# Extra products from constants in TensorE's planned pauses (a two-layer adaLN network, one core)

## Chip, core and metric

One core of a Trainium2 chip. The metric is the time of one execution in microseconds on the device. Times of several executions are given as their median. Five engines work side by side, each through its own queue in order: TensorE (PE), VectorE (DVE), ScalarE (ACT), GpSimd (POOL) and SyncE (SP), which here issues most DMAs.

## What is computed

Two layers on x of shape (16, 512, 128), float32. In each layer the input is normalised over its 128 features and scaled and shifted by amounts that depend on the batch entry; a mixer is applied; the result is multiplied by a gate and added.

```python
mod = (_silu(L0_c) @ L0_wmod).reshape(16, 6, 1, -1)        # sa, ca, ga, sb, cb, gb
h = _layernorm(x) * (1 + ca) + sa
x = x + ga * linear_attention(h)      # 16 heads of 8, causal, features elu + 1
h = _layernorm(x) * (1 + cb) + sb
x = x + gb * channel_mix(h)           # h mixed with the token before it, sigmoid gate, relu squared
# layer 1, with its own mod
h = _layernorm(x) * (1 + ca) + sa
x = x + ga * retention(h)             # 16 heads, decay, norm of each head, silu gate
h = _layernorm(x) * (1 + cb) + sb
y = _layer_norm(h + attention(h)) * g1 + be1    # over the batch entries of one time step, 4 heads
z = y + experts(y)                    # 8 experts, each token goes to the one of the highest logit
x = x + gb * (_layer_norm(z) * g2 + be2)
```

## The kernel before

The work has two parts. In the first, the 16 batch entries go through both layers up to the last normalisation, one entry (512 tokens) to a block. `both_layers` (L1086) is the program of one block: `linear_attention` (L857), `channel_mix` (L910), `retention` (L945). In the second, 16 blocks of another cut of the tokens go through `attention` (L1209) and `route` (L1407), which writes each token's row to the region of its expert in DRAM by an indirect DMA; `expert_tile` (L1602) then reads 256 rows of one expert at a time, applies it and writes the rows out by an indirect DMA.

The order of all instructions is fixed when the program is built. Each block is a Python generator that yields what it does next, "P1.9" for about 1.9 us of TensorE, "A0.8" for ScalarE, "V" for VectorE, "G" for GpSimd, "S" for SyncE, "D" for a delay. `queued` (L166) keeps, for every engine, the planned time up to which it is taken (`until`), picks the generator that can start first, and lets it issue its instructions. `now[0]` is the planned time. Five blocks run at once in the first part (`WIDTH`), seven in the second (`NROW`). The two parts are two calls of `queued`, the first at L1123, the second at L1756, each with a plan that starts at zero; between them the pools of the first part are closed and those of the second opened.

PSUM has eight banks, each 128 x 512 float32. `banks` (L271) takes some from the front of the list `free_banks`, `back` (L288) puts them at its end when the instruction that reads them has been issued in the plan. `bank_at(n)` (L248) makes a tile in bank n; an instruction that writes it waits for the last reader of that bank.

The start: the weights `wa_mod` (in `shared`) and `wa_sb` come on ScalarE's queue; on SyncE's queue come x of blocks 0 and 1, `wb_mod`, the vectors, the constants `con` (L320), x of blocks 2 to 4 and the rest. TensorE's first products are those of `modulation` (L428), from `wa_mod` and the conditioning; then the transposes in `turned` (L575), then, after ScalarE's scale and shift (L577), the products for queries and keys (L870). The chain that fills x of a block into ScalarE's queue is `normed` (L562).

The names of lines used below: L614 is `by_token`, four or more 128x128 products; L685 transposes keys; L817 and L799 are the products with states and values, after them come L840 (transposes in `closed`) and L849 (the sum into x by VectorE). In the second part L1231 transposes rows, L1234 copies them (`hb`), L1239 makes queries and keys, L1255 and L1257 spread the keys, L1292 makes the scores, L1342 applies them to the values, L1358 closes attention; L1633, L1646, L1666 and L1681 are an expert's transposes and products.

Of the kernel before, what the change touches and what calls it, by code (L numbers as in the profile page):

```python
# [29 lines left out]
P = 128  # L30
B, T, C = 16, 512, 128
# [4 lines left out]
NBLK = 16  # L36
# [12 lines left out]
SPACE, SPACE2 = 5.0, 5.0  # L49
# [5 lines left out]
NTILE, NW, NIN, NHID = 7, 5, 6, 3  # L55
NBANK = 8
NVAL, NATT = 3, 2
ND = P // DUO
LN_EPS = 1e-5
DEN_EPS = 1e-6  # L60
# [8 lines left out]
NROW = 7  # L69
# [93 lines left out]
        return at, self.next.endswith("-"), self.rank, self.ready  # L163


def queued(chains, apart, width, rank=lambda n: n, now=[0.0], side=(), behind=0):  # L166

    chains, whole, begin, free = iter(chains), [], 0.0, 0.0
    running = [Chain(steps, 0.0, -1) for steps in side]
    until = dict.fromkeys("PVAGS", 0.0)
    count = 0
    while True:
        while len(whole) < width and (steps := next(chains, None)) is not None:
            chain = Chain(steps, max(begin, free), rank(count))
            count += 1  # L180
            whole.append(chain)
            running.append(chain)
            begin = chain.ready + next(apart)
        if not running:
            return
        first = min(running, key=lambda chain: chain.start(until))
        now[0] = first.start(until)[0]
        if first.next:
            engine, us = first.next[0], float(first.next[1:].rstrip("-"))
            if engine in until:  # L190
                until[engine] = now[0] + us
            first.ready = now[0] + us + 0.1
        first.next = ""
        took = next(first.steps, None)
        if took is None:
            running.remove(first)
            if first in whole:
                first.ended = True
                while whole and whole[0].ended:
                    free = max(free, whole.pop(0).ready)  # L200
            elif first.of is not None:
                first.of.parts -= 1
                first.of.ready = max(first.of.ready, first.ready)
                if first.of.parts == 0:
                    running.append(first.of)
        elif isinstance(took, Begun):
            running += [Chain(steps, first.ready, first.rank + behind) for steps in took]
        elif isinstance(took, str):
            first.next = took
        else:  # L210
            first.parts = len(took)
            running.remove(first)
            running += [Chain(steps, first.ready, first.rank, first) for steps in took]
# [3 lines left out]
def tile_adaln(ctx: ExitStack, tc: tile.TileContext, x, wa, wb, vec, wex, const, out):  # L217
    nc = tc.nc
    mm = nc.tensor.matmul
# [19 lines left out]
    con = cp.tile([P, K_COS], F32, name="con")  # L239
# [8 lines left out]
    def bank_at(n):  # L248
        return p1.tile([P, T], F32, tag=f"bank{n}", name="bank")
# [10 lines left out]
    free_values, free_sets, now = [], [], [0.0]  # L260
    free_banks = list(range(NBANK))
# [26 lines left out]
    def back(*tiles):  # L288
        for t in tiles:
            free_banks.append(held.pop(id(t))[0])  # L290

    X, here, done = {}, {}, set()

# [44 lines left out]
    def v(i):  # L338
        return vec_sb[:, i : i + 1]
# [39 lines left out]
    def blanks():  # L379
        yield "G1.4"  # L380
        make_identity(nc, ident)
        nc.gpsimd.memset(lneps, LN_EPS)
        nc.gpsimd.memset(eps4, LN_EPS)
        nc.gpsimd.memset(power, -0.5)
        nc.gpsimd.memset(minus, -1.0)
        yield "G1.8"
        for t in values:
            nc.gpsimd.memset(t, 1.0)
        free_values.extend(range(NVAL))
        yield "G1.0"  # L390
        nc.gpsimd.memset(avg, 1.0 / C)
        nc.gpsimd.memset(keep, 1.0)
        nc.gpsimd.memset(keep[:, :, 0:1], 0.0)
        for n in range(NATT):
            yield "D%.1f" % (5.0 + 14.0 * n)
            yield "G1.1-"
            nc.gpsimd.memset(states[n], 0.0)
            free_sets.append(n)

    def blank_values():  # L400
        for n in range(NVAL):
            engine = nc.gpsimd if n else nc.vector
            yield "G1.1-" if n else "V1.1-"
            engine.memset(v_chunks[n], 0.0)
            yield "G2.1-" if n else "V2.1-"
            engine.memset(v_heads[n], 0.0)
            done.add(("blank", n))
            yield "D%.1f" % max(0.0, BLANKS + 8.0 * n - now[0])
# [45 lines left out]
    def gates():  # L454
        yield [
            modulation(0, wa_mod, 4.5, [(0, 1), (2, 3, 4, 5)]),
            modulation(1, wb_mod, LATER, [tuple(range(6))]),
        ]
        yield "V0.6-"
        ts(omu, mu, -1.0, 1.0, ALU.mult, ALU.add)  # L460
        gbe2 = cp.tile([P, B], F32, name="gbe2")
        ts(gbe2, mod1[:, 5, :], v(V_BE2), None, ALU.mult)
        gg2 = cp.tile([P, B], F32, name="gg2")
        ts(gg2, mod1[:, 5, :], v(V_G2), None, ALU.mult)
        shift = cp.tile([P, B], F32, name="shift")
        ts(shift, mod1[:, 3, :], v(V_BO), None, ALU.add)
        of_entry = (mod0[:, 2], mod0[:, 5], mod1[:, 2], gbe2, mod1[:, 4], shift, gg2)
        got = yield from banks(2)
        yield "P1.6"
        for n, m in enumerate(of_entry):  # L470
            nc.tensor.transpose(got[n // 4][0:B, n % 4 * C : (n % 4 + 1) * C], m, ident)
        yield "V1.2"
        mod_sb = of_set(NATT - 1, [P, RG, T], "sc").rearrange("p r t -> p (r t)")[0:B, 0 : NMOD * C]
        for n, ps in enumerate(got):
            at = slice(4 * n * C, min(NMOD, 4 * n + 4) * C)
            nc.vector.tensor_copy(mod_sb[:, at], ps[0:B, 0 : at.stop - at.start])
        back(*got)
        yield "S0.5"
        nc.sync.dma_start(out=mod_rows, in_=mod_sb)
        here["rows"] = now[0] + 2.5  # L480
        done.add("omu")
        yield "D20.0"
        for n in range(GRP):
            yield "S0.5"
            nc.sync.dma_start(out=gain[n * B : (n + 1) * B], in_=mod_rows[:, NGATE * C :])

    def end_weights():
        yield "D%.1f" % (LATER - 1.0)
        yield "V0.6-"
        nc.vector.tensor_copy(wend[:, 0], wa_col(A_PROJ))  # L490
        ts(wend[:, 1], wa_col(A_V), 0.5, None, ALU.mult)
        ts(wend[:, 2], wb_mod[:, B_O : B_O + C], 0.5, None, ALU.mult)
        done.add("wend")

    def turned_weights():
        yield "D20.0"
        yield "V0.7"
        tt(cen, ident, avg, ALU.subtract)
        ts(cen_h, blk, -1.0 / HD, None, ALU.mult)
        tt(cen_h, cen_h, ident, ALU.add)  # L500
        ps = yield from bank()
        yield "P0.4"
        nc.tensor.transpose(ps[:, 0:C], wb_col(B_V), ident)
        yield "V0.3"
        nc.vector.tensor_copy(wvt, ps[:, 0:C])
        yield "P0.5"
        mm(ps[:, C : 2 * C], lhsT=wvt, rhs=cen_h, start=True, stop=True)
        yield "V0.3"
        nc.vector.tensor_copy(wv1, ps[:, C : 2 * C])
        back(ps)  # L510
        done.add("turned")
# [563 lines left out]
    def blank_rows():  # L1075
        yield "D60.0"
        blank = con[:, K_NONE + 1 - R_END : K_NONE + 1]
        for e in range(NE + 1):
            yield "S0.7"
            nc.sync.dma_start(  # L1080
                out=sorted_rows[e * REGION : e * REGION + TS].rearrange("(p a) k -> p a k", a=2),
                in_=blank.unsqueeze(1).to_broadcast([P, 2, R_END]),
            )
            yield "D8.0"

    def both_layers(b):  # L1086
# [40 lines left out]
        lambda n: min(n, 2 * LATE - n),  # L1127
        now,
        side=[gates(), blanks(), blank_values(), end_weights(), turned_weights(), blank_rows()],
    )  # L1130
    order.close()
    blocks.close()
# [32 lines left out]
    for n in range(2):  # L1165
        t = wk.tile([P, 4 * ND, MH, DUO], F32, name=f"k_own{n}", bufs=1)
        nc.gpsimd.memset(t, 0.0)
# [575 lines left out]
    def attend_and_route(i):  # L1743
        k, n, first = of_block[i]
        row = yield from attention(i)
        if k not in logits:
            logits[k] = wk.tile([P, MOST_G, NE], F32, tag="logits", name="logits", bufs=4)[:, 0 : 4 * n]
            ready[k] = 0
        at = 4 * (i - first)
        yield from normed_rows(i, row, logits[k][:, at : at + 4])  # L1750
        ready[k] += 1
        if ready[k] == n:
            yield Begun([route(k, first, n, logits[k])])

    with tc.manual_schedule():
        queued((attend_and_route(i) for i in range(NBLK)), repeat(SPACE2), NROW, now=now, behind=4)  # L1756


# [90 lines left out]
```

## Time and profile before

| | |
|---|---|
| median of 3 runs | 1036.85 us (1034.77 to 1041.96) |
| the profiled execution, its own time | 1042.77 us |
| its span, first to last instruction | 1040.7 us |
| TensorE busy | 848.7 us (82%), 16319 records |
| VectorE, ScalarE, GpSimd busy | 722.6, 719.9, 586.7 us |
| mean granted clock of TensorE | 0.923 |
| HBM traffic | 65.94 MB read, 38.51 MB written |

The profile is of one execution. Busy time is the time in which an engine has an instruction in it; records of TensorE's products overlap a little, since they are pipelined. A row of a timeline gives the start in us, the length in us, engine and line, operation, output and inputs, the count that was merged, and in brackets how long the engine had been idle and what ended that. The granted clock is the share of full speed that TensorE was given; in the stretches of this trace it is 1.0 or 0.5. The part of the chain of waits in an engine's name is time in which that engine's work was what the end waited for.

### The profile page before, as it was taken

How to read it: one execution, taken by the hardware profiler on the slowest of the kernel's cores; microseconds unless marked ns; L12 is line 12 of the kernel's file. 1: busy time of each engine (PE TensorE's matmuls, PEld its weight loads, DVE VectorE, ACT ScalarE, POOL GpSimd, SP SyncE). 2: the span in 40 equal slices, each digit the busy share in tenths (PEclk: the TensorE clock that was granted, in tenths of full speed). 3: DMA queues.
4: the chain of work that ended last, by engine and by line, in shares of the span. 5: the costliest groups of instructions: out<-in, count | busy, mean ns of one | idle time of the engine just before them, and what ended most of it. 6: DMA issues, size and time to landing. Idle time of an engine off the chain costs nothing.

```text
span 1040.7 us, 39498 instructions
## 1 busy us (share of the span) xinstructions
PE 848.7 (82%) x16319; PEld 632.2 (61%) x16319; DVE 722.6 (69%) x2183; ACT 719.9 (69%) x1437; POOL 586.7 (56%) x782
## 2 busy tenths in 40 slices
PE   6798887888998889888888988478668678868985
PEld 4566665666766656666665656346445556646874
DVE  6466876666777778666697667658779688756454
ACT  6666676887868688876678667159768677634664
POOL 6316648544555765636375574244762575775576
PEclk9799988899999999999899889789789999978998
DMA  6634324153422333525133032230365564568763
GB/s 202 155 71 113 75 60 111 49 128 69 107 62 51 80 73 88 114 46 115 35 76 71 23 77 51 60 125 1 126 199 172 168 212 142 182 187 285 227 190 100
DMA packets 147555, 116.52 MB, mean 112 GB/s; under 512 B 75269, under 2 KB 127240, under 8 KB 147248
## 3 DMA queue, kind: packets, MB, share of 16 engines
q1 hardware_dynamic: 140720, 96.05, 35.9%
q0 software_dynamic: 6368, 17.08, 4.4%
q8 instruction: 129, 2.11, 0.9%
q10 hardware_dynamic: 288, 0.86, 0.3%
q14 instruction: 50, 0.41, 0.1%
HBM read 65.94 MB, written 38.51 MB: 100 GB/s over the span
## 4 chain that ended last, share of the span: by engine, by line
PE 35%; ACT 17%; DVE 17%; POOL 10%; issue 9%; DMA 9%; SPq 2%; POOLq 0%; another core or an unknown queue 0%; ACTq 0%; DVEq 0%
PE bank L614 5%; PE bank L1646 4%; DMA v_rows<-values 3%; PE bank L817 3%; PE bank L1666 3%; PE bank L765 3%; PE bank L799 3%; ACT q L562 3%; PE bank L780 2%; PE bank L698 2%; PE bank L870 2%; ACT kh L664 1%; POOL rs L532 1%; POOL out_x L1722 1%; DVE k_own L1255 1%
## 5 line engine op out<-in xcount | busy, mean ns | idle before, releaser
L562 ACT ACTIVATE q<-x,off,rs 128x128 f32<-128x128 f32 x244 | 100.3, 484 | 35.8 <-POOL off L559 31.6
L1722 POOL DMA_INDIRECT out_x<-z,l_to x71 | 71.9, 1013 | 38.2 <-issue 13.7
L774 ACT COPY sc<-bank 128x512 f32<-128x512 f32 x128 | 68.1, 585 | 34.5 <-PE bank L765 34.2
L747 DVE TENSOR_TENSOR sc<-bank,con 128x512 f32<-128x512 f32 x128 | 82.1, 681 | 11.3 <-PE bank L780 9.9
L765 PE MATMUL bank<-kh,q 32*32 32x128 f32 x4096 | 81.7, 281 | 9.4 <-issue 6.0
L735 POOL COPY states<-added 32x576 f32<-32x576 f32 x64 | 46.9, 732 | 67.8 <-DVE added L720 65.2
L664 ACT ACTIVATE kh<-k,con 128x512 f32<-128x512 f32 x128 | 81.8, 715 | 0.1
L1646 PE MATMUL bank<-y,w 128*128 128x256 f32 (+1 forms) x312 | 75.5, 387 | 5.6 <-ACT y L1636 3.6
L1656 ACT ACTIVATE hid<-bank,w 128x256 f32<-128x256 f32 (+1 forms) x156 | 60.4, 462 | 26.5 <-PE bank L1646 13.9
L780 PE MATMUL bank<-ident,sc 128*128 128x128 f32 x512 | 74.7, 292 | 3.2 <-DVE x L849 1.2
L765 PEld LDWEIGHTS bank<-kh,q 32*32 32x32 f32 x4096 | 60.8, 107 | 26.1 <-issue 11.2
L799 PE MATMUL bank<-v_heads,sc 128*32 128x36 f32 x4096 | 60.5, 202 | 16.4 <-issue 9.8
L1666 PE MATMUL bank<-hid,w 128*128 128x256 f32 (+1 forms) x312 | 70.6, 372 | 2.6 <-ACT hid L1656 2.2
L799 PEld LDWEIGHTS bank<-v_heads,sc 128*32 128x32 f32 x4096 | 47.3, 111 | 41.5 <-issue 25.6
L956 POOL TENSOR_TENSOR th<-th,trig 128x512 f32<-128x512 f32 x32 | 43.1, 1347 | 47.4 <-DVE th L972 41.6
L614 PE MATMUL bank<-gated,h 128*128 128x128 f32 x384 | 60.9, 309 | 10.9 <-DVE h L1018 6.7
L532 POOL TENSOR_TENSOR rs<-rs,power 128x4 f32<-128x4 f32 x64 | 66.1, 1033 | 5.0
L780 PEld LDWEIGHTS bank<-ident,sc 128*128 128x128 f32 x512 | 60.6, 149 | 11.2 <-ACT sc L774 3.8
L1646 PEld LDWEIGHTS bank<-y,w 128*128 128x128 f32 x312 | 56.4, 201 | 17.3 <-ACT y L1636 6.9
L531 POOL TENSOR_TENSOR rs<-mv,eps 128x4 f32<-128x4 f32 x64 | 17.2, 269 | 88.2 <-DVE mv L525 77.2
L614 PEld LDWEIGHTS bank<-gated,h 128*128 128x128 f32 x384 | 53.2, 215 | 18.2 <-DVE h L1018 6.8
L1666 PEld LDWEIGHTS bank<-hid,w 128*128 128x128 f32 x312 | 55.6, 195 | 10.7 <-ACT hid L1656 3.9
(285 smaller groups left out, 2325.2 us busy)
## 6 DMA issues: line engine op xcount, KB each, us to landing
w<-in_wex SPq DMA_DIRECT2D x39, 514.5 KB
x_in<-sorted_rows SPq DMA_DIRECT2D x32, 393.0 KB
v_rows<-values SPq DMA_DIRECT2D x32, 288.0 KB
v_chunks<-values SPq DMA_DIRECT2D x128, 72.0 KB
v_heads<-v_rows SPq DMA_DIRECT2D x128, 72.0 KB
rows<-token_rows SPq DMA_DIRECT2D x13, 512.0 KB
gated<-mod_rows SPq DMA_DIRECT2D x16, 384.0 KB
x<-in_x SPq DMA_DIRECT2D x16, 256.0 KB
```

The costliest lines, as they stand in the source:

```text
L532: nc.gpsimd.tensor_tensor(rs, rs, power, ALU.pow)
L562: nc.scalar.activation(xn[:, g, :], X[b][:, g, :], AF.Identity, bias=off[:, g : g + 1], scale=rs[:, g : g + 1],)
L614: mm(groups(ps)[:, g, :], lhsT=groups(src)[:, g, :], rhs=w, start=True, stop=True,)
L664: nc.scalar.activation(t[:, :, n, :], k.rearrange("p (n s) -> p n s", s=CH), AF.Copy, scale=con[:, K_HEAD + n : K_HEAD + n + 1],)
L747: tt(sc[:, rr + 2 * r].rearrange("p (n t) -> p n t", t=CH), t.rearrange("p (n t) -> p n t", t=CH), causal.unsqueeze(1).to_broadcast([P, NC ...
L765: mm(groups(s_ps[r])[c * CH : (c + 1) * CH, n], lhsT=by_block[rows, at], rhs=kh[rows, at].rearrange("p m s -> p (m s)"), start=True, stop= ...
L774: nc.scalar.copy(sc[:, rr + 2 * r], s_ps[r])
L780: nc.tensor.transpose(groups(st_ps[r])[:, n], groups(sc[:, rr + 2 * r])[:, n], ident)
L799: mm(o_ps[a][c * CH : (c + 1) * CH, k0 : k0 + RH * HV], lhsT=groups(sc[:, r])[:, g, c * CH : (c + 1) * CH], rhs=vh[:, g * NC + c, :, r * H ...
L1646: mm(h_ps[d][:, f % 2 * n : (f % 2 + 1) * n], lhsT=w[:, E_W1 + f * P : E_W1 + (f + 1) * P], rhs=y, start=True, stop=True,)
L1666: mm(o_ps[:, 0:n], lhsT=w[:, E_W2 + f * C : E_W2 + (f + 1) * C], rhs=hid[f // 2][:, f % 2 * n : (f % 2 + 1) * n], start=f == 0, stop=f == ...
L1722: sent = nc.gpsimd.indirect_dma_start(out=out_rows, out_offset=bass.IndirectOffsetOnAxis(ap=to[:, a : a + 1], axis=0), in_=z[:, a], in_off ...
```

## The change

`queued` gets a function `idle`. When the step that it is about to issue is TensorE's, and TensorE's planned time lies at least 1.05 us back, it calls `idle` with that pause first. The function, `kept_awake`, looks whether a bank is free, and if so issues int((pause - 0.5) / 0.55) products of 128 x 128 by 128 x 512 from the constants into the bank at the front of the list. The bank stays in the list, and nothing reads the products. The plan itself (`until`, `now`) isn't changed by them. Both calls of `queued` get it, and ahead of the second one it is called once with 8.0 us, which makes thirteen products.

```diff
+IDLE = 1.05
...
-def queued(chains, apart, width, rank=lambda n: n, now=[0.0], side=(), behind=0):
+def queued(chains, apart, width, rank=lambda n: n, now=[0.0], side=(), behind=0, idle=None):
...
             engine, us = first.next[0], float(first.next[1:].rstrip("-"))
+            if engine == "P" and idle and now[0] - until[engine] >= IDLE:
+                idle(now[0] - until[engine])
             if engine in until:
                 until[engine] = now[0] + us
...
+    def kept_awake(us):
+
+        if free_banks:
+            spare = bank_at(free_banks[0])
+            for _ in range(int((us - 0.5) / 0.55)):
+                mm(spare, lhsT=con[:, 0:P], rhs=con[:, 0:T], start=True, stop=True)
...
         side=[gates(), blanks(), blank_values(), end_weights(), turned_weights(), blank_rows()],
+        idle=kept_awake,
     )
...
     with tc.manual_schedule():
-        queued((attend_and_route(i) for i in range(NBLK)), repeat(SPACE2), NROW, now=now, behind=4)
+        kept_awake(8.0)
+        queued((attend_and_route(i) for i in range(NBLK)), repeat(SPACE2), NROW, now=now, behind=4, idle=kept_awake)
```

In the program that comes of it the other engines' instructions stand in the same order as before. TensorE has 77 products more, at 24 places: ten ahead of the first product of L428 and one inside that group; 3, 1, 1, 1 and 4 in the rest of the first part; 16 at the hand-over (the thirteen and three of the first planned pause); 40 in the second part, in groups of 1 to 10.

## The prediction

> **What bounds the kernel now.** I read the page first, then the start, the hand-over between the two planned parts, the chain of waits around every place where products are added, and last the granted clock by stretch.
>
> ```profile
> span 1040.7 us, 39498 instructions
> PE 848.7 (82%) x16319; PEld 632.2 (61%) x16319; DVE 722.6 (69%) x2183; ACT 719.9 (69%) x1437; POOL 586.7 (56%) x782
> PE 35%; ACT 17%; DVE 17%; POOL 10%; issue 9%; DMA 9%; SPq 2%; POOLq 0%; another core or an unknown queue 0%; ACTq 0%; DVEq 0%
> ```
>
> TensorE is the fullest engine and holds the largest share of the chain, but only about a third: no engine bounds the whole, and a microsecond added to TensorE costs a microsecond only where the chain passes it. The start, from the timelines of SyncE's queue, TensorE, ScalarE and VectorE:
>
> ```profile
> 3.16 0.62 SPq L320 DMA_DIRECT2D con<-in_const  x1
> 7.04 2.74 PE L428 MATMUL bank<-mod_sg,shared 128*128 128x16 f32 x12 [7.04 <-DVE mod_sg L422]
> 7.79 0.87 DVE L523 BATCH_NORM_STATS2 st<-x 128x6 f32<-128x128 f32 x4 [0.81 <-DMA x<-in_x]
> 10.81 0.49 DVE L523 BATCH_NORM_STATS2 st<-x 128x6 f32<-128x128 f32 x2 [1.56 <-DMA x<-in_x]
> 12.34 1.44 ACT L577 ACTIVATE h<-bank,mod 128x512 f32<-128x512 f32 x2
> 13.15 3.78 PE L870 MATMUL bank<-h,wa_sb 128*128 128x512 f32 x4 [0.19 <-ACT h L577]
> ```
>
> TensorE's first real work (L428) starts at 7.04. The constants are requested on SyncE's queue between the second and the third block's x, whose statistics start at 7.79 and 10.81, when those blocks land. And a 128x512 product of float32 is two records, not one: L980 has 32 records for 16 blocks. Two products fill those 3.78 us: at full clock two take 1.98.
>
> The hand-over, in TensorE's timeline, with one later row to compare:
>
> ```profile
> 663.32 3.27 PE L614 MATMUL bank<-gated,h 128*128 128x128 f32 x16 [0.18 <-DVE h L1018]
> 676.17 0.45 PE L1231 MATMUL bank<-ident,shared 128*128 128x128 f32 x1 [9.58 <-DMA shared<-q]
> 678.55 3.78 PE L1239 MATMUL bank<-hb,wb_sb 128*128 128x512 f32 x4 [0.80 <-ACT hb L1234]
> 687.90 1.98 PE L1239 MATMUL bank<-hb,wb_sb 128*128 128x512 f32 x4 [0.68 <-ACT hb L1234]
> ```
>
> 9.58 us of nothing, and the same four records then take 3.78 us where they later take 1.98. That is what the change is after. Its worth at most, from the windows of the eight half-clock stretches that lie beside added products:
>
> ```profile
> 730.80:737.60 6.80, 5.39 (x71) 4.45 (x72) 4.51 (x13) 5.24 (x11) 5.98 (x7) 0.50 0.25 91
> 932.20:945.80 13.60, 6.85 (x19) 4.93 (x18) 10.98 (x45) 4.31 (x10) 10.32 (x13) 0.50 0.89 300
> sum 68.10, PE 45.72 PEld 33.86 DVE 42.00 ACT 30.78 POOL 41.28; mean PE 5.72 PEld 4.23 DVE 5.25 ACT 3.85 POOL 5.16
> ```
>
> The columns are busy time of TensorE, its loads, VectorE, ScalarE, GpSimd, then the granted clock. Of 68.1 us at half clock TensorE is busy for 45.7: half of it, 22.9 us, is the most that a full clock could give back there.
>
> **What the change adds.** The instruction order of the other engines is unchanged; TensorE gets 77 products at 24 places, in plan order. Each is a 128x512 product of float32. Price: two products start to start took 1.82 us at full clock (L1239 at 687.90, L1267 at 689.72), so 0.9 each; 3.58 us at the slow clock of the start (L870 at 13.15, L428 at 16.73), so 1.8 each. The code's rule, (us - 0.5)/0.55, gives each 0.55 us. So every run of several products lasts about 1.6 times the plan's pause, and the plan's pause isn't the trace's.
>
> *The start: ten products ahead of L428, one inside it.* They wait for the constants. These land between 7.8 and 10.8; 797 KB (second weights 456, vectors 6, constants 335) of the 1053 KB between those two marks are ahead of their end, so at 7.8 + 3.0 x 0.76 = 10.1 us. L428, ready at 7.04, stands behind them. The page prints clock 1.00 for the first 20 us, but the 3.78 us of L870 says half. Dense work brought the full clock after 4.3 us there (13.15 to about 17.4) and 6.8 us at the hand-over (676.2 to 683.0). So 2.4 to 3.8 products at 1.8, the rest at 0.9: 11.1 to 12.4 us, ending near 22. Then two of L428's products (0.6), the eleventh extra (0.9), four more (1.2), the first block's transposes (0.6): L577 starts near 25 instead of 12.34, 12.7 us late. Behind L577 in ScalarE's order stand the second block's L577 and L562 of the third block. ScalarE is busy 15.97 of the 17.66 us from 12.34 to 30, so it wins back 1.7 at most, and every queue then carries the shift, since the planned order is fixed. I take +10.5. Bounds: +6 (a pipeline that is still filling wins back half) to +13.
>
> *First part, elsewhere.* Three products at 162.9 have no pause there (2.7 us of TensorE), but the chain runs through the DMA of v_rows from 162.2 to 169.4: +0.5, bounds 0 to 2.7. Single products at 199.5, 591.5, 605.3 lie in pauses of 2.77, 0.85, 1.83: nothing; without that cover 0.9 each. Four at 660.5 lie in a pause of 2.12 from 658.4. The clock goes to half at 659.1 because of the pause before it, so they end near 663.7, 3.1 late; afterwards L840 (1.09 to 0.6) and L614 (3.27 to 2.3) run at full clock: +1.5, bounds 0 to 3.
>
> *The hand-over: sixteen products* (thirteen written out, three from the first planned pause). They wait for VectorE's and ScalarE's last reads of the old bank, so from about 667.3 (L849). At 0.9 they end at 681.7; the transposes needed at 676.2 end at 682.4, hb at 683.0, L1239 at 685.05 instead of 682.4. So the cure of L1239 is paid for and more: +2.6, and up to +6 if the first 3.4 to 6.8 us are at half clock. I take +3.
>
> *Second part: 40 products, single and in groups, from 698.9 on.* Against the pauses found at the same places they overrun by: three at 730.7, 0.7 (pause 2.00); seven at 741.7, 2.5 (3.77); ten at 938.7, 2.9 (6.09); three at 761.2, 1.5; two at 782.5, 0.6; three at 852.8, 1.6; two at 900.6, 1.4; five singles that meet hardly any pause (746.5, 754.2, 917.0, 949.1, 1025.0), 3.8; the others are covered. That is 15.0 us. Given back where the clock becomes full: L1342 and L1292 at 730.7 and 734.1 (1.93 to 1.08 each), L1358 (2.00 to 1.09), L1342 and L1358 after 741.7 (1.94 to 1.08, 2.18 to 1.09), together 4.6; at 938.7 L1646 (3.78 to 1.99), L1666 (2.81 to 1.99), the transposes 0.25, together 2.8. The chain passes TensorE at those two places, so 6.1 of overrun against 7.4: -1.3. Of the other 8.9 the chain there runs by turns through VectorE, SyncE, GpSimd and TensorE; I count half: +4.4. Sum +3. Bounds -4 (only a third of the 8.9 counts, with one of the savings more) to +10 (all of the overrun, half of the savings).
>
> Sum: 10.5 + 0.5 + 1.5 + 3 + 3 = +18.5. The profiled execution took 1042.77 us around its span of 1040.7, 5.9 above the median of 1036.85: 1061.3 on its scale, 1055 on the median's. Low ends together 6 + 0 + 0 + 2.6 - 4 = +5, near 1041. High ends 13 + 2.7 + 3 + 6 + 10 = +35; all at once is too much, so 1069.
>
> [...] The row first: TensorE's pauses of 2.15 and 2.12 us around 657 were enough for the half clock from 659.1 on. [...]
>
> **Rivals.** *The clock wins.* All eight half-clock stretches run at full clock on the path: -22.9. For: TensorE has the largest share of the chain. Against: the chain at 669 to 683 and 932 to 946 is largely DMA, VectorE and GpSimd. With the start at +10.5 and half of the 15.0 overrun that is -4.9: 1032, not slower. It decides from about 18 us saved on the path, four fifths of the bound. *The start's hold is lost in the filling pipeline.* For: ScalarE is busy only 12.45 of the 20 us from 30 to 50. Against: the shift reaches every queue alike. 18.5 - 10.5 = +8: 1045. *It doesn't do what it says:* products placed by plan miss the real pauses, the clock still falls after them, and only the overrun is left: 18.5 + 7.4 + 3 (slow products) = +29: 1066.
>
> **How the numbers follow.** Forecast 0.64, missed pauses 0.20, lost hold 0.11, clock wins 0.05. The runs before differ by 0.7%, so 1% (10.4 us) is about what can be told from no change. The forecast and the missed pauses are slower; the lost hold is within 1%, with 0.03 of the clock's; 0.02 of it and 0.01 for the unknown are faster: 0.03, 0.14, 0.83. The range 1041 to 1069 leaves out the clock's win and the top of the missed pauses.
>
> **What would show it.** Ten products of two records each from 10 us to about 22, L577 at 25; sixteen from 667 (plus the shift) that last over 14 us, and the first L1231 after them with no wait for its DMA; 154 more records on TensorE and some 65 to 75 us more busy time; L1239 at 2.0 at the hand-over; the end of the first part 11 to 14 us later. I am wrong if the first L428 still starts near 7, if a product lasts half of 0.9, or if the shift of L577 is gone by 100 us.

## The result, and the profile after

The changed kernel took 1050.83 us (median of 4 runs, 1045.44 to 1056.99) against 1037.06 for the kernel before (4 runs): 1.0118 times the time of before, 95% interval 1.0076 to 1.0161, or +12 us (8 to 17). The same kernel beside fresh runs of before gave 1.0138 (1.0099 to 1.0177). It is slower, as forecast, by two thirds to three quarters of the 18.5 us of the sum. All ratios here leave out executions over 1.5% above the fastest of the same kernel; in the second of the three studies below one execution of before, at 1009.78 us, draws that line at 1024.9 and so leaves out 14 of its 29, which is why the four experiments of that study also carry the difference of the means of all executions.

Line numbers of the changed kernel are 10 higher than before in the first part and 11 higher in the second; the new products are L300. From its page, then its TensorE timeline at the start, the hand-over and two places of the second part, then ScalarE's timeline at the start:

```profile
span 1043.4 us, 39802 instructions
PE 889.4 (85%) x16473; PEld 642.5 (62%) x16473; DVE 722.1 (69%) x2183; ACT 720.1 (69%) x1437; POOL 588.5 (56%) x782
PEclk9999999989999999999998988999989999999998
PE 39%; DVE 17%; ACT 16%; POOL 11%; issue 9%; DMA 6%; SPq 1%; POOLq 0%; DVEq 0%; ACTq 0%
L300 PE MATMUL bank<-con 128*128 128x512 f32 x154 | 74.1, 621 | 14.0 <-DMA con<-in_const 9.6
```

```profile
9.56 11.42 PE L300 MATMUL bank<-con 128*128 128x512 f32 x20 [9.56 <-DMA con<-in_const]
20.82 0.51 PE L438 MATMUL bank<-mod_sg,shared 128*128 128x16 f32 x4
24.44 1.98 PE L880 MATMUL bank<-h,wa_sb 128*128 128x512 f32 x4 [0.43 <-ACT h L587]
...
664.15 13.97 PE L300 MATMUL bank<-con 128*128 128x512 f32 x32 [0.87 <-DVE x L859]
677.96 0.60 PE L1242 MATMUL bank<-ident,shared 128*128 128x128 f32 x4
679.36 1.98 PE L1250 MATMUL bank<-hb,wb_sb 128*128 128x512 f32 x4 [0.80 <-ACT hb L1245]
...
735.10 6.17 PE L300 MATMUL bank<-con 128*128 128x512 f32 x14
741.21 1.08 PE L1353 MATMUL bank<-att_own,vt 128*32 128x128 f32 x32
...
934.89 8.75 PE L300 MATMUL bank<-con 128*128 128x512 f32 x20
943.47 0.38 PE L1644 MATMUL bank<-ident,x_in 128*128 128x128 f32 x2
944.51 1.99 PE L1657 MATMUL bank<-y,w 128*128 128x256 f32 x8 [0.66 <-ACT y L1647]
```

```profile
23.61 1.45 ACT L587 ACTIVATE h<-bank,mod 128x512 f32<-128x512 f32 x2 [11.52 <-PE bank L585]
```

Three things are to be seen. The products do what they are for: the granted clock of the execution is 0.959 instead of 0.923, and nearly every row behind products is at full clock (1.98, 1.08, 1.99 where before had 3.78, 1.94, 3.78); the exceptions are the single product at 198.67 (the L624 behind it took 1.91) and the pair at 764.60 (L1353, 1.64). They are also paid in full: 154 records are 77 products and took 74.1 us, while TensorE's busy time rose by only 40.7 us, so some 33 us of shorter rows did not make the kernel faster. The missing bracket after "x4" at 677.96 and "x2" at 943.47 says that real work no longer waits for its DMA but stands directly behind products. And the constants now release TensorE's first instruction, at 9.56, and so hold ScalarE's L587 for 11.52 us.

### The profile page after: what moved, and what is told of

Same layout as the page of the kernel before. It is cut to its first block, busy times and chain, and to the rows that moved or that the text cites. A ratio compares the mean times of both kernels' runs of the same rounds, so it can differ in the third digit from the quotient of the medians.

```text
span 1043.4 us, 39802 instructions
## 1 busy us (share of the span) xinstructions
PE 889.4 (85%) x16473; PEld 642.5 (62%) x16473; DVE 722.1 (69%) x2183; ACT 720.1 (69%) x1437; POOL 588.5 (56%) x782
## 4 chain that ended last, share of the span: by engine, by line
PE 39%; DVE 17%; ACT 16%; POOL 11%; issue 9%; DMA 6%; SPq 1%; POOLq 0%; DVEq 0%; ACTq 0%
PE bank L624 4%; PE bank L300 4%; PE bank L1657 3%; PE bank L775 3%; PE bank L790 3%; PE bank L1677 3%; PE bank L809 3%; PE bank L827 3%; ACT q L572 2%; PE bank L1250 2%; PE bank L708 2%; POOL rs L542 1%; POOL out_x L1733 1%; ACT kh L674 1%; DMA v_chunks<-values 1%
## 5 line engine op out<-in xcount | busy, mean ns | idle before, releaser
L300 PE MATMUL bank<-con 128*128 128x512 f32 x154 | 74.1, 621 | 14.0 <-DMA con<-in_const 9.6
L790 PEld LDWEIGHTS bank<-ident,sc 128*128 128x128 f32 x512 | 61.0, 150 | 11.3 <-issue 2.5
L624 PE MATMUL bank<-gated,h 128*128 128x128 f32 x384 | 54.8, 288 | 9.5 <-DVE h L1028 5.1
```

What stands on the lines that cost most here:

```text
L300: mm(spare, lhsT=con[:, 0:P], rhs=con[:, 0:T], start=True, stop=True)
L624: mm(groups(ps)[:, g, :], lhsT=groups(src)[:, g, :], rhs=w, start=True, stop=True,)
L790: nc.tensor.transpose(groups(st_ps[r])[:, n], groups(sc[:, rr + 2 * r])[:, n], ident)
```

## Experiments

Every kernel was timed beside the kernel before on the same chip. Before's median was 1023.8, 1024.8 and 1037.5 us in the three studies, so only the ratios are compared; a difference in us below is the ratio times that median, with its 95% interval.

**The start alone, and all but the start.** The callbacks of the two calls of `queued` are limited by planned time:

```diff
# e1: start alone
-        idle=kept_awake,
+        idle=lambda us: kept_awake(us) if now[0] < 10.0 else None,
...
-        kept_awake(8.0)
-        queued((attend_and_route(i) for i in range(NBLK)), ..., behind=4, idle=kept_awake)
+        queued((attend_and_route(i) for i in range(NBLK)), ..., behind=4)
# e2: all but the start
-        idle=kept_awake,
+        idle=lambda us: kept_awake(us) if now[0] > 10.0 else None,
```

> Only the eleven products at the start are kept (ten ahead of the first L428, one inside it); none in the rest of the first part, at the hand-over or in the second part. Theory of the prediction (the start's hold reaches the end): L577 starts some 11 us late and the whole is 8 to 11 us slower than before. Rival (the shift is won back within the first part, as the profile of the changed kernel suggests, where it fell from 11 us at 25 us to 5 at 55 and to none at 200): within 4 us of before. A shift still seen at 100 us and gone at 650 would say that it is lost in stretches of half clock that the executions don't share.

> The eleven products at the start are left out, the other 66 are kept (10 in the first part, 16 at the hand-over, 40 in the second part). Theory of the prediction: +8 of the +18.5 us is left, so 4 to 8 us slower than before and 6 to 10 faster than the changed kernel. Rival (the start's hold is won back): as slow as the changed kernel, 12 to 14 us over before.

Measured: the start alone 1.0072 (1.0043 to 1.0102), +7.4 us (4.4 to 10.4), a little under the 8 to 11 expected. All but the start 1.0047 (1.0017 to 1.0076), +4.8 us (1.7 to 7.8). Together 12.2, which is what the whole costs. So by these values the larger part of the loss is eleven products of the 77 (the two intervals overlap), and the rival, that the shift is won back, falls. It had looked right in the traces: set against the trace of before, instruction by instruction on ScalarE, the changed kernel was 9.8 us late at 25 us, 4.4 late at 53 and not late at 200. But one trace of before does not carry that. Four kernels of these experiments have no product in the first part, and at 53 us they stand 4.9 (thirteen at the hand-over only), 4.5 (second part only), 5.4 (eight at the hand-over) and 1.4 us (sized) ahead of it. Its execution had a granted clock of 0.51 from 27.6 to 34.5 and again from 48.1 to 55.0. Against the four the start alone is 6.7 to 10.7 us late at 53 and 6.3 to 12.8 at 650. The shift was not won back; the one trace of before was slow there.

**How the start's length counts.** The same eleven from a tile that GpSimd fills, so that they wait for no DMA; and twice as many from the constants:

```diff
# e6, on top of e1
+    warm = cp.tile([P, T], F32, name="warm")
+    nc.gpsimd.memset(warm, 0.5)
...
-                mm(spare, lhsT=con[:, 0:P], rhs=con[:, 0:T], start=True, stop=True)
+                mm(spare, lhsT=warm[:, 0:P], rhs=warm, start=True, stop=True)
# e7, on top of e1
-        idle=lambda us: kept_awake(us) if now[0] < 10.0 else None,
+        idle=lambda us: (kept_awake(us), kept_awake(us)) if now[0] < 10.0 else None,
```

> Only the eleven products at the start, as in the run with the start alone, but from a tile that GpSimd fills first, so that they wait for no DMA and begin near 1.5 us. Theory A (what costs is that L428 stands behind them, in us of delay): ten products from 1.5 us end near 13, L577 starts near 16.5, 4 us late instead of 11, and the whole is 2 to 4 us over before, against 7 with the wait for the constants. Theory B (the number of products costs, whenever they run): 7 us over before. Theory C (an early full clock pays): faster than before by 2 us or more.

> Only the start's products, twice as many: twenty ahead of L428 and two inside it. They should last 9.5 us longer than eleven, so L577 starts near 33.5, 21 us late. Theory A (a fixed few us of the hold are won back in the first 60 us, the rest reaches the end): +7.4 and 9.5 more, 16 to 17 us over before. Theory B (a fixed share of the hold is won back, about a third): 14 us over. Theory C (the pipeline has slack, and most of the hold is lost whatever its length): under 10 us over before.

ScalarE's timelines of the early, the single and the double start, in that order (the line is `turned`'s scale and shift; its number moves with the lines added):

```profile
15.46 1.45 ACT L589 ACTIVATE h<-bank,mod 128x512 f32<-128x512 f32 x2 [3.21 <-PE bank L587]
```

```profile
23.95 1.45 ACT L587 ACTIVATE h<-bank,mod 128x512 f32<-128x512 f32 x2 [11.73 <-PE bank L585]
```

```profile
33.95 1.45 ACT L587 ACTIVATE h<-bank,mod 128x512 f32<-128x512 f32 x2 [21.62 <-PE bank L585]
```

Holds of 3.2, 11.7 and 21.6 us became +4.0 (-0.2 to 8.3), +7.4 (4.4 to 10.4) and +27 (21 to 34). By the means of all executions the early start is +0.4 (-2.6 to 3.4) and the double one +21 (17 to 25). The early start kept the products and lost most of the wait. By the means it costs less than the 7 us of theory B, so the delay counts and not the number of products; the first interval alone would still allow 7. The hope for an early full clock falls too (its L882, L870 of before, took 1.99 instead of 3.78, and nothing was gained). For the double start all three expectations were too low: nearly the whole hold, or all of it, reaches the end. A fixed loss of some 3 us would fit all three holds by the means and not by the ratios; what share of a hold is won back stays open.

**The hand-over alone, with thirteen and with eight products.**

```diff
# e3: no callbacks; e11: the same with
-        kept_awake(8.0)
+        kept_awake(0.6 + 0.55 * 8)
```

> Only the thirteen products written out at the hand-over are kept. They should last 11.2 us at 0.86 each, from the last read of the old banks: 0.7 us after the last L614 to about 2 us after the rows have landed, so L1231 is up to 2 us late, but L1239 takes 2.0 instead of 3.8: the start of L1255 within 1 us of before, the whole within 2 us of before. Rival (the full clock after the hand-over is worth more than L1239): 3 us or more faster. Other rival (the products' wait for the banks costs): 3 us or more slower.

> Only the hand-over, with 8 products instead of 13. They last 6.9 us and end 1.8 us before the rows land, so L1231 waits for its DMA again and nothing is late; L1239 takes 2.0 us if the clock holds through the 1.8 us. Theory of the prediction: 1.5 to 2 us faster than before, too little to be told from no change; the start of L1255 1.8 us earlier after the last L614 than before (15.8 us in the trace of before, 14.0 here). Rival: L1239 at 3.8 all the same, since the clock falls in the remaining pause.

Thirteen: 0.9994 (0.9969 to 1.0020). Eight: 1.0010 (0.9978 to 1.0042). TensorE's timeline with thirteen:

```profile
664.54 11.40 PE L300 MATMUL bank<-con 128*128 128x512 f32 x26 [0.87 <-DVE x L859]
676.00 0.66 PE L1241 MATMUL bank<-ident,shared 128*128 128x128 f32 x4
677.45 1.98 PE L1249 MATMUL bank<-hb,wb_sb 128*128 128x512 f32 x4 [0.80 <-ACT hb L1244]
...
682.66 1.08 PE L1302 MATMUL bank<-k_own,q 128*32 128x128 f32 x32 [2.30 <-ACT k_own L1267]
...
685.13 3.78 PE L1249 MATMUL bank<-hb,wb_sb 128*128 128x512 f32 x4 [0.68 <-ACT hb L1244]
```

The first L1249 is cured and the second is ill. The clock fell after the next pause, 2.30 us (granted clock 1.00 from 677 to 682 us, 0.66 from 682 to 692), and the half clock that before had on the first block's products now lies on the second's. With eight it was not even moved: L1249 took 3.78 at once, behind a pause of 1.59 us:

```profile
672.34 0.30 PE L1241 MATMUL bank<-ident,shared 128*128 128x128 f32 x1 [1.59 <-DMA shared<-q]
674.50 3.78 PE L1249 MATMUL bank<-hb,wb_sb 128*128 128x512 f32 x4 [0.80 <-ACT hb L1244]
```

The start of L1255 after the end of the last L614, 15.85 us before, is 15.88 with thirteen, 15.61 with eight and 18.17 with the change's sixteen, the last in all three traces that have them (the changed kernel twice, and all but the start).

**Second part alone.** No callback in the first part, none at the hand-over:

```diff
-        idle=kept_awake,
...
-        kept_awake(8.0)
-        queued((attend_and_route(i) for i in range(NBLK)), ..., behind=4, idle=kept_awake)
+        queued((attend_and_route(i) for i in range(NBLK)), ..., behind=4, idle=lambda us: kept_awake(us) if now[0] > 10.0 else None)
```

> Only the 40 products in the second part; none in the first part, none at the hand-over. Theory of the prediction: +3 us, from 15 us of overrun, of which half is on the path, less what the full clock gives back at two places; 1 to 5 us over before. Rival (the 4.8 us that the run without the start's products was over before come from the first part and the hand-over): within 1.5 us of before. Other rival (the full clock pays there): 2 us or more faster.

Measured 1.0045 (1.0002 to 1.0088), +4.6 us (0.2 to 9.0), but by the means of all executions +0.5 (-2.4 to 3.4). So what the second part costs is not shown; it may be the whole of the 4.8 us of all but the start or next to nothing. The clock did rise there (mean granted clock 0.941 against 0.927 to 0.929 before), and no gain of 3 us or more came of it.

**Half as wide.** All 77 products with 256 columns, then the same without the start's eleven:

```diff
-                mm(spare, lhsT=con[:, 0:P], rhs=con[:, 0:T], start=True, stop=True)
+                mm(spare[:, 0 : T // 2], lhsT=con[:, 0:P], rhs=con[:, 0 : T // 2], start=True, stop=True)
```

> All 77 products are kept, but each has 256 columns instead of 512, so that one lasts about 0.43 us, near the 0.55 that the planned pauses are divided by. Theory of the prediction (the overrun is what costs, since a product lasts longer than the rule gives it): the ten at the start end near 16.5 instead of 21, the sixteen at the hand-over before the rows land, the overrun in the second part falls from 15 to some 3 us, and the whole is 0 to 5 us over before. Rival (what costs is that products stand where the trace has no pause, whatever their length): over 8 us slower than before. Third (the clock pays once the overrun is gone): faster than before by 3 us or more.

> The products of 256 columns as in the run with half width, but without the eleven at the start: 66 products that last about 0.43 us and fit the planned pauses. Theory A (the half-width run at +1.2 us was what its start cost, L577 6 us late, less a little that the clock gave): 2 to 4 us faster than before. Theory B (a full clock in the pauses is worth nothing, since the chain waits elsewhere): within 2 us of before.

Measured 1.0012 (0.9984 to 1.0040) with the start, 1.0017 (0.9978 to 1.0056) without; by the means of all executions the second is -2.2 us (-4.8 to 0.4). One edit of the length takes the change from +1.2% to nothing that can be told: the overrun is what costs, as the first theory said. Whether something is gained with it gone is open. With the start, L587 is still held for 6.17 us; without it, a gain of 2 to 4 us is inside both intervals (the first is -2.3 to +5.7 us) and shown by neither.

**Sized to the trace.** 8 products at the hand-over, 4, 3 and 6 at the three long pauses of the second part, nothing else:

```diff
+    places = {4: 4, 9: 3, 14: 6}
+    calls = [-1]
+
+    def sized(us):
+        if not free_banks or int((us - 0.5) / 0.55) < 1:
+            return
+        calls[0] += 1
+        if calls[0] in places:
+            kept_awake(0.6 + 0.55 * places[calls[0]])
```

> Only the places where the trace of before has a pause over 3.4 us in front of work at half clock or near it, each with as many full products as end before the next real one: 8 at the hand-over (pause 9.58), 4 ahead of the L1342 at 741.7 (3.77), 3 ahead of the one at 771.0 (3.99), 6 ahead of the L1633 at 938.7 (6.09). Nothing at the start. Theory of the prediction (the savings of 1.8, 1.9 and 2.8 us at the hand-over, 741.7 and 938.7 are real and were only hidden by the overrun): 3 to 7 us faster than before. Rival (the clock falls again in the next pause, so the half clock is moved and not removed): within 2 us of before, with the next work at the hand-over, the second L1239, at 3.8 us in the profile.

Measured 1.0012 (0.9985 to 1.0039), +1.2 us (-1.6 to 4.0). The 3 to 7 us of the theory lie outside, and the rival's second L1239 at 3.8 is there. TensorE's timeline at the hand-over and at the last of the places:

```profile
670.46 1.98 PE L1259 MATMUL bank<-hb,wb_sb 128*128 128x512 f32 x4 [0.80 <-ACT hb L1254]
...
680.91 3.78 PE L1259 MATMUL bank<-hb,wb_sb 128*128 128x512 f32 x4 [0.68 <-ACT hb L1254]
...
927.00 5.32 PE L300 MATMUL bank<-con 128*128 128x512 f32 x12
933.49 0.41 PE L1653 MATMUL bank<-ident,x_in 128*128 128x128 f32 x2 [1.18 <-DMA x_in<-sorted_rows]
934.56 3.33 PE L1666 MATMUL bank<-y,w 128*128 128x256 f32 x8 [0.66 <-issue]
```

The products end in time at both places, and both times half clock follows all the same: at the hand-over behind a pause of 3.88 us (granted clock 0.51 from 677 to 686 us, 3.78 on the second L1239), at the last place behind what is left of the pause, 1.18 us, and the next one of 0.66 (3.33 on the first expert products, where the changed kernel has 1.99). At the two places between, L1342 starts 0.1 and 0.3 us after its input is ready and runs at full clock (1.08). After the first of them the half clock comes two pauses later (L1239 takes 3.44 at 744.36); after the second the next L1239, at 771.00, takes 1.88.

At the hand-over a second wait ends close behind the cured row. VectorE clears `att_own` (L1170) just ahead of L1255; first the trace of before, then the sized one:

```profile
680.08 1.76 DVE L1170 MEMSET att_own<- 128x2048 f32 x1 [0.37 <-issue]
682.44 1.51 DVE L1255 TENSOR_SCALAR k_own<-bank,b_qkv 32x512 f32<-32x512 f32 x2 [0.59 <-PE bank L1239]
...
672.36 1.76 DVE L1190 MEMSET att_own<- 128x2048 f32 x1 [0.38 <-issue]
674.14 1.52 DVE L1275 TENSOR_SCALAR k_own<-bank,b_qkv 32x512 f32<-32x512 f32 x2
```

In before, VectorE waits only 0.59 us for L1239. In the sized run that wait is gone and L1255 starts 15.28 us after the last L614 instead of 15.85 (15.28 also in the half-wide kernel with the start, where the first L1239 takes 1.98 too): of the 1.8 us by which the row got shorter, 0.6 reach the next step.

The sized run and the one with eight have the same eight products here and the same pause behind them (1.60 and 1.59 us), and yet one has its first L1239 at 1.98 and the other at 3.78. So the length of the pause does not tell them apart; what does is not shown.

**The changed kernel again.**

> The changed kernel itself, once more beside the sized ones. If its parts add up, it is 7.4 (the start alone) and 4.8 (all but the start) over before, 12 us or 1.2%, with the interval of its first measurement, 0.8 to 1.6%. Rival (the start's hold and the rest overlap, or one feeds the other): under 9 or over 16 us.

Measured 1.0138 (1.0099 to 1.0177), +14.3 us (10.3 to 18.4): the start alone and all but the start, 12.2 together, add up to it within the intervals.

## Why the prediction held, point by point

*Price of a product: right.* Sixteen took 13.81 us, from 664.15 to 677.96, so 0.86 each; taken 0.9. That a product is two records, and the code's 0.55 us too little for it, decided the sign: at half the width the loss was gone.

*The start, mechanism right, size too large.* The constants released TensorE at 9.56 (taken 10.1), the ten ended near 20.8 (taken 22), L577 started at 23.61 (taken 25), 11.3 us late instead of 12.7. What reaches the end was taken as +10.5; the start alone measured +7.4 (4.4 to 10.4), 3 us less. The bound of +6, a filling pipeline that wins back half, was not needed; the double start shows no such slack.

*The rest of the first part and the hand-over: right at the hand-over, too large before it.* They were +5. The hand-over's sixteen were sized right: L1255 starts 18.17 us after the last L614 instead of 15.85, +2.3 against +2.6. The four at 660.5 were not: forecast at half clock with +1.5, they ran at full clock in 3.5 us (655.49 to 659.03), and from the end of L817 to the end of L614 it took 7.7 us instead of before's 8.2. The other two traces with the four also have 7.7, and those with no product in the first part 8.2 to 8.7, so here the products gained about half a microsecond to one.

*The second part: size not shown.* Forecast +3, measured +4.6 (0.2 to 9.0) by one count and +0.5 (-2.4 to 3.4) by the other. At 741.7 the step can be read. ScalarE's copies for L1342 in the changed kernel are

```profile
737.55 2.53 ACT L1346 COPY att_own<-att 32x512 f32<-32x512 f32 x4 [1.73 <-DVE att L1340]
```

They end at 740.08, and L1342 starts at 741.21, behind the seven products of 6.1 us: 1.1 us late, where 2.5 was forecast. The shorter rows give that back (L1342 1.08 for 1.94, L1358 1.19 for 2.18). Two bounds of this term do not come out of their own words: a third of the 8.9 and one more saving of 4.6 give about -3, not -4, and the whole overrun with half of the savings about +11, not +10.

*Which term failed most in its reason: what the clock gives back.* The sum credited about 7.4 us in the second part, and 1.8 within the hand-over's term, for rows at full clock. The rows did become shorter. But the sized kernel, which should have shown that gain bare, shows none (1.0012). Its hand-over shows why: the half clock moved to the next pause, and VectorE stood 0.6 us behind the row that was cured, so the 1.8 us could not pass. In the half-wide one without the start the mean granted clock rose from 0.929 to 0.942, and the time fell by 2.2 us by one count and not at all by the other. All but the start had 0.955 against 0.927 and was slower.

*Signs that did not come.* TensorE's busy time was to rise by 65 to 75 us; the products took 74.1, but the total rose by 40.7, since the real rows became shorter. The first part was to end 11 to 14 us later; the last L614 ends at 663.28 in one trace of the changed kernel and at 668.90 in the other, against 666.59 in before's trace. Single traces can't carry this sign: without any product in the first part that end lies between 658.9 and 666.6.

*Rivals.* "The clock wins" (1032 us) fell with the result, and the sized run shows no gain either. "The hold is lost in the filling pipeline" (1045) fell with the start alone and the double start. "Products miss the real pauses and only the overrun is left" (1066) is too high, though its first half is what the sized run shows at the hand-over.

*Places by the length of their pause: not to be had.* The forecast read pauses of 2.15 and 2.12 us as enough for the half clock from 659.1 on. The later traces show no length that settles it. The same pause of 2.30 us ahead of L1292 left the clock full on the second block's L1239 in the changed kernel (1.98) and was followed by half clock with thirteen products alone (3.78); a pause of 1.59 us was followed by half clock (3.78) and one of 1.60 us was not (1.98). The 3.4 us by which the sized run's places were picked was the author's choice, and no run shows it as a bound.

## What to carry to other kernels

Before filling an engine's pauses with extra work, price that work from a row of the same shape and type, and price the instruction that stands behind it: here eleven products ahead of the first real one cost 7.4 us and the other 66 cost 4.8. Ask what they wait for, too; a filler that waits for a later DMA than the work behind it turns an idle engine into a late one (here TensorE started at 9.56 us instead of 7.04, and L577 at 23.61 instead of 12.34). And a clock that is kept up for one pause can fall in the next (with thirteen products L1239 took 1.98 on the first block and 3.78 on the second), so the value of a fuller clock is the time saved in a run with fillers that fit, not the rows that got shorter. Look also at how long the next engine waits for the slow row: that wait, here 0.59 us, is the most that a shorter row can give while the other engine's own work stays where it is.

## What the runs showed of the hardware

At the hand-over the granted clock of before was 0.50 from 659.1 to 665.9 us, around a pause of TensorE of 2.12 us, and 0.50 again from 669.4 to 683.0, from inside the pause of 9.58. In the changed kernel, whose products stand in both pauses, it was 1.00 from 659.3 to 678.0, and L1239 took 1.98 us instead of 3.78.

How long the single pause was does not say what came behind it. With eight products alone TensorE was idle for 1.59 us, ran the first L1231 (0.30), and the other three took 0.68 and L1239 3.78. In the sized run the idle time was 1.60 us, the first L1231 took 0.30 too, the other three 0.55 and L1239 1.98; there the rows are slow only behind the next pause, 3.88 us (L1292 1.93 for the 1.08 it takes in the run with eight). What sets the two executions apart is not shown.

Executions of one order of instructions differ by several us: four of before took 1034.77 to 1041.96 us. In the third study before took 1029.11 us at a mean granted clock of 0.934 and 1041.49 us at 0.919.

The granted clock printed for the first 15 us is 1.00, while L870 at 13.15 took 3.78 us (1.98 in the changed kernel, at 24.44), so a duration and not the column tells the clock there.
